# Cross-attention and gated FFN on one core: zero products during the first loads, another order of loads, and both ends of the attention reordered

## The chip, the core and the metric

The kernel runs on one core of one Trainium2 chip, in float32. The metric is the device time of one execution in microseconds; the number for the kernel before is the median of three runs, 1118.73 us (1117.19 to 1122.49). The engines are TensorE (PE; its weight loads are shown as PEld), VectorE (DVE), ScalarE (ACT), GpSimd (POOL) and SyncE (SP, which here only starts transfers). [...]

## The reference, cut to what matters

B = 8 blocks of S = 128 tokens, D = 512, H = 32 heads of 128; the FFN has 1376 inner columns.

```python
def reference(x, ctx_4096, mask_BxSxS2_bk0, position_bias, ln_weight, w_q, w_k, w_v, w_out, Wg, Wu, Wd, ag, au, ad):
    # hidden = layernorm(x)
    q = (rmsnorm(hidden) * ln_weight) @ w_q.T          # [B, S, 32, 128]
    k, v = ctx @ w_k.T, ctx @ w_v.T                    # [B, S, 32, 128]
    score = einsum('bqhd,bkhd->bhqk', q, k) + position_bias
    score = where(mask, softmax(where(mask, score, -inf)), 0)
    attn = einsum('bhqk,bkhd->bqhd', score, v)
    x = x + hidden + attn @ w_out.T
    # y = layernorm(x)
    x = x + ((silu((y @ Wg.T) * ag) * ((y @ Wu.T) * au)) @ Wd.T) * ad
```

## The kernel before

The 32 heads are worked on in NG = 8 groups of GH = 4 heads (512 columns). The host lays weights and context out with the contracted axis first. All large products are done by a seven-product scheme (Strassen-Winograd): each operand is cut into quarters, sums and differences of quarters are formed beforehand, and seven products of halves take the place of eight. `sums_a` (L220) and `sums_b` (L228) form the four sums of an operand, in place where they can. `combine_rows` (L236) does this on GpSimd for a group's weights, `token_sums` (L244) for the context and for the normalised tokens. `seven` (L259) runs the seven products for two output tiles each, so 14 steps, in the order 2, 1, 6, 7, 4, 5, 3. Products 2, 6, 7 and 4 are copied out of PSUM by ScalarE (L270, L280), products 1, 5 and 3 are added by VectorE (L275, L286). Product 6 accumulates into the bank of product 1, 7 into that of 6, 4 into that of 7, and 3 into that of 5: each must wait until the result before it has been read out of the bank. In the trace a matmul call in float32 shows as two records.

The stages follow one another on TensorE. First `kv(0, ...)` (L410) makes keys and values of group 0 in 28 steps while the loads come in; between the steps, at counts given by hand (L440 to L449), the blocks of x are normalised: `norm1_moments` (L186: statistics on VectorE, a square root on ScalarE), `norm1_scale` (L198: two small VectorE operations, the scaling on ScalarE) and `norm1_T` (L207: four transposes on TensorE, a multiplication on VectorE into hT). The sums of hT follow. Next come the queries of all eight groups (L541, L485 and L296), which are stored to DRAM. Then the attention runs over groups g = 0 to 7 and blocks b = 0 to 7. In each step `probabilities` (L327) adds position bias and mask on GpSimd into a tile s (three buffers, L332), makes the scores on TensorE (L337), adds them to s and takes the maximum on VectorE (L340 to L344), and makes four exponentials on ScalarE (L347) and the division on VectorE; `transpose_p` (L369) transposes in squares of 32 on VectorE and turns the rest with one store and four loads through DRAM (`turned`, then `pT`, all on SP's queue). Three steps later `attend` (L391) multiplies with the values, and ScalarE copies and stores the result (`att`). Between the steps TensorE makes three or four of the 28 steps of the next group's keys and values (`products`, counts at L687); before the first step it makes three. In group 7, whose successor has no keys, the steps of the output projection for the first two blocks (`first_out`, `out_products` at L618) stand in their place. `attended` (L605) loads a group's attended values for two blocks and forms their sums on VectorE; `load_wo` (L582) loads a group's rows of the output weights and forms their sums on GpSimd. Afterwards the output projection of the other three pairs of blocks follows, with residual and normalisation, and then the FFN.

A scheduler orders the instructions of each engine's queue by its own estimate of when each is ready, over what the program's order and the data allow; the hardware then works through each queue strictly in that order. Instructions given through `InOrder` (L37) are pinned behind whatever instruction was written just before them for the same engine. In the kernel before this holds for VectorE and GpSimd up to the queries, for TensorE during the first four steps of attention, and for TensorE and VectorE in group 7.

## Time and profile before

| what | value |
|---|---|
| median of three runs | 1118.73 us (1117.19 to 1122.49) |
| profiled execution | 1120.01 us, of it the program's span 1118.2 us |
| TensorE busy | 1093.8 us (98%), granted clock 0.997 over the span |
| VectorE, ScalarE, GpSimd busy | 571.4, 314.1, 373.7 us |
| group 0's keys and values | 4.4 to 63.9 us |
| queries | 63.9 to about 247 us |
| attention | 247 to about 761 us |
| rest of output projection, FFN | 761 to 1118 us |

A row of instructions gives the line, the engine, the operation, the tiles written and read, the shape and the count; in the order of time it begins with start and length in microseconds, and the brackets hold the idle time before it and what ended that. A row of waits says who waited for whom: microseconds in total, how often, and the longest. The chain of work that ended last is followed back from the end of the stretch asked for. A row of windows gives, for a stretch of time, its length and the busy time (and number) of PE, PEld, DVE, ACT and POOL, then the granted TensorE clock, the share of DMA and GB/s. TensorE counts as busy from the start of a matmul to its modelled end, so half speed looks busy too. SPq, ACTq and POOLq are the queues' own instructions, such as the start of a transfer.

### The profile page before, as it was taken

To read this page: it belongs to the slowest core of one execution; us is meant where nothing else is said; L and a number is where in the kernel's file an instruction comes from. 1 tells how busy PE (TensorE), PEld (TensorE's weight loads), DVE (VectorE), ACT (ScalarE), POOL (GpSimd) and SP (SyncE) were. 2 spreads that over 40 slices of the span, in tenths; PEclk is the share of its full clock that TensorE was granted. 3 is DMA by queue.
4 is the path that set the end of the run, shared out by engine and by line. 5 is a ranking of instruction groups with operands and counts; after the bars stand their busy time and mean duration, and the time that the engine had idled before them with its cause. 6 is when DMAs were issued, how large, how long until landed. Compare 5 with 4: busy or idle time off the path is not lost.

```text
span 1118.2 us, 13138 instructions
## 1 busy us (share of the span) xinstructions
PE 1093.8 (98%) x4526; PEld 775.1 (69%) x4526; DVE 571.4 (51%) x1122; ACT 314.1 (28%) x880; POOL 373.7 (33%) x386
## 2 busy tenths in 40 slices
PE   7999999998999999999999999998999999999998
PEld 4656666654868778685968778887888864444687
DVE  4664444436555565555555666643444333434732
ACT  2422211114444443434444344221000012223100
POOL 5283335535333333322311733620000316930010
PEclk9999999999999999999999999998999999999999
DMA  9113344448555555556545557664222512110011
GB/s 284 51 38 113 113 155 183 151 177 275 171 161 173 168 177 169 179 181 187 167 157 178 168 179 237 225 213 156 94 86 84 188 59 76 38 38 0 1 38 38
DMA packets 117538, 154.44 MB, mean 138 GB/s; under 512 B 12032, under 2 KB 71680, under 8 KB 117472
## 3 DMA queue, kind: packets, MB, share of 16 engines
q1 hardware_dynamic: 104416, 128.95, 36.2%
q10 hardware_dynamic: 11408, 18.88, 4.8%
q0 software_dynamic: 1648, 5.77, 1.6%
q8 instruction: 36, 0.59, 0.2%
q14 instruction: 30, 0.25, 0.1%
HBM read 101.14 MB, written 52.43 MB: 137 GB/s over the span
## 4 chain that ended last, share of the span: by engine, by line
PE 88%; DMA 4%; DVE 3%; POOL 2%; issue 1%; ACT 1%; SPq 0%; ACTq 0%; POOLq 0%; DVEq 0%
PE mm_v L314 16%; PE mm_k L296 14%; PE m L627 13%; PE mm_f L916 10%; PE mm_q L485 9%; PE d L995 6%; PE av L395 4%; PE sc L337 4%; PE ia_q L541 3%; PE ib_q L541 2%; PE mm_q L296 2%; DMA wo<-in_woT_dram 2%; DMA a<-att 1%; PE mm_k L45 1%; DMA wv<-in_wvT_dram 1%
## 5 line engine op out<-in xcount | busy, mean ns | idle before, releaser
L332 POOL TENSOR_TENSOR s<-pb,mneg 128x512 f32<-128x512 f32 x64 | 81.4, 1275 | 274.1 <-DVE tt L372 228.9
L314 PE MATMUL mm_v<-wv,ctx_sb 128*128 128x256 f32 x512 | 118.2, 379 | 1.4 <-DMA wv<-in_wvT_dram 1.4
L296 PE MATMUL mm_k<-ctx_sb,wk 128*128 128x512 f32 x224 | 105.0, 602 | 6.5 <-DMA wk<-in_wkT_dram 4.4
L347 ACT ACTIVATE s<-s,nmx 128x128 f32<-128x128 f32 x252 | 98.0, 390 | 44.6 <-DVE nmx L344 29.5
L314 PEld LDWEIGHTS mm_v<-wv,ctx_sb 128*128 128x128 f32 x512 | 94.5, 190 | 14.4 <-DMA wv<-in_wvT_dram 2.2
L314 PE MATMUL mm_v<-S_v,ctx_sb 128*128 128x256 f32 x384 | 86.6, 380 | 3.3 <-DVE v L45 1.7
L400 ACT COPY aT<-av 128x512 f32<-128x512 f32 x64 | 37.5, 587 | 183.2 <-PE av L395 142.1
L314 PEld LDWEIGHTS mm_v<-S_v,ctx_sb 128*128 128x128 f32 x384 | 71.9, 190 | 14.1 <-DVE v L45 2.3
L296 PE MATMUL mm_k<-ctx_sb,S_k 128*128 128x512 f32 x168 | 75.1, 592 | 0.0
L627 PE MATMUL m<-wo,a 128*128 128x256 f32 x300 | 74.3, 386 | 0.0
L337 PEld LDWEIGHTS sc<-k,q 128*128 128x128 f32 x416 | 58.7, 191 | 20.2 <-issue 18.2
L340 DVE TENSOR_TENSOR s<-sc,s 128x512 f32<-128x512 f32 x56 | 38.7, 691 | 65.3 <-PE sc L337 61.1
L296 PEld LDWEIGHTS mm_k<-ctx_sb,wk 128*128 128x128 f32 x224 | 40.4, 193 | 44.4 <-issue 34.8
L493 ACT COPY q<-mm_q 128x512 f32<-128x512 f32 x56 | 31.4, 588 | 121.5 <-PE mm_q L485 111.8
L627 PEld LDWEIGHTS m<-wo,a 128*128 128x128 f32 x300 | 57.6, 194 | 7.8
L545 DVE TENSOR_TENSOR q<-q,ia_q 128x256 f32<-128x256 f32 x84 | 34.9, 421 | 52.6 <-PE ia_q L541 51.7
L337 PE MATMUL sc<-k,q 128*128 128x128 f32 x416 | 59.0, 275 | 0.0
L296 PEld LDWEIGHTS mm_k<-ctx_sb,S_k 128*128 128x128 f32 x168 | 31.2, 190 | 35.4 <-issue 34.0
L395 PE MATMUL av<-pT,v 128*128 128x128 f32 x416 | 55.0, 275 | 0.0
L485 PE MATMUL mm_q<-hT,S_q 128*128 128x512 f32 x112 | 52.3, 592 | 0.0
L485 PE MATMUL mm_q<-hT,wq 128*128 128x512 f32 x112 | 52.3, 592 | 0.0
L395 PEld LDWEIGHTS av<-pT,v 128*128 128x128 f32 x416 | 50.6, 192 | 0.0
(251 smaller groups left out, 1940.7 us busy)
## 6 DMA issues: line engine op xcount, KB each, us to landing
queries<-q SPq DMA_DIRECT2D x32, 512.0 KB, 3.5
q<-queries SPq DMA_DIRECT2D x32, 512.0 KB, 4.8
turned<-tt SPq DMA_DIRECT2D x64, 256.0 KB, 2.1
pT<-turned SPq DMA_DIRECT2D x256, 64.0 KB, 2.6
att<-aT ACTq DMA_DIRECT2D x64, 256.0 KB, 3.1
a<-att SPq DMA_DIRECT2D x24, 512.0 KB, 3.3
wq<-in_wqT_dram SPq DMA_DIRECT2D x8, 1024.0 KB, 5.3
wk<-in_wkT_dram SPq DMA_DIRECT2D x7, 1024.0 KB, 6.2
```

The costliest lines, as they stand in the source:

```text
L296: kv_tensor.matmul(out, w[i][:, c, bass.ts(t, P)], src[i][:, c, :], start=(first and c == 0), stop=(c == HC - 1), skip_group_check=True,)
L314: kv_tensor.matmul(out[:, bass.ts(k, HW)], src[i][:, c, bass.ts(2 * t + k, S)], w[i][:, c, :], start=(first and k == 0 and c == 0), stop=( ...
L332: nc.gpsimd.tensor_tensor(s, pb, mneg[:, b : b + 1, :].to_broadcast([P, GH, S]), ALU.add)
L337: tensor.matmul(sc[:, j, :], qT[:, j, bass.ts(b % 2, S)], kT[j][:, cols], start=True, stop=True)
L340: vector.tensor_tensor(s, sc, s, ALU.add)
L347: (InOrder(tc, nc.scalar) if (g, b) == (0, 0) else nc.scalar).activation(s[:, j, :], s[:, j, :], AF.Exp, bias=nmx[:, j : j + 1], accum_out ...
L395: tensor.matmul(av[:, j, :], v[b // 2][:, b % 2, bass.ts(j, P)], pT[:, :, j, :], start=True, stop=True,)
L485: nc.tensor.matmul(m[t], w[i][:, c, bass.ts(t, P)], h_t[i][:, c, :], start=(i in (1, 5) and c == 0), stop=(c == HC - 1), skip_group_check= ...
L541: nc.tensor.matmul(m, a[n][i], b[n][i], start=i in (2, 1, 5), stop=True, skip_group_check=True)
L627: tensor.matmul(m[n], sa[n][:, c, :], wo_t[g][n][:, c, :], start=(g == order[0] and c == 0 and k % 2 == 0), stop=(g == order[-1] and c == ...
L916: nc.tensor.matmul(out, ws[t][n][:, c, :], h2_t[n][:, c, :], start=(first and c == 0), stop=(c == HC - 1), skip_group_check=True,)
L995: nc.tensor.matmul(out, lhs, rhs, start=bank not in started, stop=(i == NP - 1 or n == 8), skip_group_check=True,)
```

## The change

At the start, eight products of a zero tile (128x128 by 128x256, into a PSUM bank of its own) are written before everything else of TensorE. The first loads come in another order: the values' weights are issued right behind the first keys' weights, and the second half of the keys' weights moves from ACT's queue to SP's, ahead of x. Keys and values of group 0 are written in the order two steps of keys, two of values, two of keys, two of values, and the values' sums only after that. ScalarE's copies and normalisations up to the queries are pinned in the order in which they are written, and the normalisation's counts change.

At the start of attention two steps of products (not three) precede the first scores, three follow each of the first six blocks, and four follow the last two. The loads of wo for groups 0 and 1 are pinned on SP behind what is written before them at groups 1 and 2, and their sums are written at block 3 of groups 1, 2 and 6.

In group 7 GpSimd and SP are pinned too. The masked bias is made two blocks ahead; attended values are loaded one block ahead from SP instead of POOL; one step of the last values' products moves between the exponentials and the sums; wo's sums are written one block after its load, and the last wo is loaded at block 4 instead of 5. The attended values of the second pair of blocks for groups 0 and 1 are loaded and summed (on GpSimd) at the end of group 7, and the first four of their seven products are written around the last two `attend`s, into banks that attention leaves. The other three follow afterwards.

```diff
@@ -132,13 +132,14 @@
     for c in (2, 3):
         nc.scalar.dma_start(wk0[:, c, lo], wkT[bass.ts(c, P), lo])
         nc.sync.dma_start(ctx_sb[:, c, :512], ctxT[bass.ts(c, P), :512])
+    load_part(nc.scalar, wv0, wvT, 1, lo)
     load_part(nc.scalar, wk0, wkT, 0, lo)
     load_part(nc.sync, ctx_sb, ctxT, 0, slice(0, 512))
+    load_part(nc.scalar, wv0, wvT, 0, lo)
     for fh in (1, 0):
-        load_part(nc.scalar, wv0, wvT, fh, lo)
         load_part(nc.sync, ctx_sb, ctxT, fh, slice(512, T))
-        load_part(nc.scalar, wk0, wkT, fh, hi)
     for fh in (1, 0):
+        load_part(nc.sync, wk0, wkT, fh, hi)
         load_part(nc.scalar, wv0, wvT, fh, hi)
     kv_w = {0: (wk0, wv0)}
     x_in = [acts.tile([P, 2, D], F32, tag="a", name=f"x_{i}") for i in range(B // 2)]
@@ -147,7 +148,14 @@
     q_w = {0: load_q(0)}
-    vector, gpsimd = InOrder(tc, nc.vector), InOrder(tc, nc.gpsimd)
+    vector, gpsimd, scalar = (InOrder(tc, e) for e in (nc.vector, nc.gpsimd, nc.scalar))
+    zeros = work.tile([P, 256], F32, tag="aT", name="zeros")
+    nc.vector.memset(zeros, 0.0)
+    zero = ps.tile([P, 256], F32, tag="av", name="zero")
+    for _ in range(8):
+        nc.tensor.matmul(zero, zeros[:, :P], zeros, start=True, stop=True)
     lnw_sb = const.tile([P, DC], F32, name="lnw_sb")
     nc.gpsimd.dma_start(lnw_sb, lnw.rearrange("(c p) -> p c", p=P))
...
@@ -192,7 +200,7 @@
         rr = small.tile([P, 1], F32, tag="rr", name=f"rr_{b}")
         vector.tensor_scalar(rr, mv1[:, b, 1:2], 1.0 + EPS, EPS * EPS, ALU.mult, ALU.add)
+        scalar.activation(rr, rr, AF.Sqrt)
         return b, rr
...
+            scalar.copy(part(1, 1, t), m[t])
             yield
...
@@ -324,14 +332,17 @@
         yield from seven(name, range(2), product, part, *banks)
-    def probabilities(g, b, qT, kT, pb, between=None):
+    def masked_bias(eng, g, b, pb):
+        s = work.tile([P, GH, S], F32, tag="s", name=f"s_{g}_{b}", bufs=3)
+        eng.tensor_tensor(s, pb, mneg[:, b : b + 1, :].to_broadcast([P, GH, S]), ALU.add)
+        return s
+    def probabilities(g, b, qT, kT, pb, between=None, s=None):
         cols = bass.ts(b, S)
         n = f"{g}_{b}"
-        s = work.tile([P, GH, S], F32, tag="s", name=f"s_{n}", bufs=3)
-        nc.gpsimd.tensor_tensor(
-            s, pb, mneg[:, b : b + 1, :].to_broadcast([P, GH, S]), ALU.add
-        )
+        if s is None:
+            s = masked_bias(nc.gpsimd, g, b, pb)
         sc = ps.tile([P, GH, S], F32, tag="sc", name=f"sc_{n}")
         for j in range(GH):
             tensor.matmul(
@@ -418,13 +429,17 @@
             yield from project_V(f"v{g}", combine_rows(f"v{g}", wv), ctx_t, v, ps_mm)
         else:
+            rows_v = {1: wv[:, :HC, :HW], 2: wv[:, HC:, :HW]}
+            values = project_V(f"v{g}", rows_v, ctx_t, v, ps, "sc")
+            yield from itertools.islice(keys, 2)
+            yield from itertools.islice(values, 2)
             ctx_sums[0]()
-            yield from itertools.islice(keys, 3)
+            yield from itertools.islice(keys, 1)
             ctx_sums[1]()
             ctx_sums[2]()
             yield from itertools.islice(keys, 1)
-            values = project_V(f"v{g}", combine_rows(f"v{g}", wv), ctx_t, v, ps, "sc")
-            yield from itertools.islice(values, 4)
+            rows_v.update(combine_rows(f"v{g}", wv))
+            yield from itertools.islice(values, 2)
             ctx_sums[3]()
             yield from keys
             yield from values
@@ -437,11 +452,11 @@
     h_t, h_sums = token_sums(hT)
     scales = []
     for n, _ in enumerate(kv(0, kvs)):
-        if n in (3, 6, 8, 9, 10, 12, 14, 16):
+        if n in (6, 7, 8, 9, 10, 12, 14, 16):
             scales.append(norm1_moments(len(scales) + len(normed) + transposed1))
-        if n in (6, 8, 9, 10, 12, 14, 16, 18):
+        if n in (8, 9, 10, 11, 12, 14, 16, 18):
             normed.append(norm1_scale(*scales.pop(0)))
-        if n in (10, 11, 12, 14, 16, 18, 20, 22):
+        if n in (10, 11, 12, 13, 14, 16, 18, 20):
             norm1_T(*normed.pop(0))
             transposed1 += 1
...
+    scalar = nc.scalar
     res_scale = const.tile([P, B], F32, name="res_scale")
     res_bias = const.tile([P, B], F32, name="res_bias")
@@ -581,54 +597,77 @@
     def load_wo(g):
         src = woT[bass.ts(g, GW), :].rearrange("(c p) n -> p c n", p=P)
...
+            sync.dma_start(w, src)
...
-        wo_t[g] = sums_b(
-            nc.gpsimd, up[:, :, :HW], up[:, :, HW:], dn[:, :, :HW], dn[:, :, HW:], t1, t2, t4
-        )
-    def attended(g, i):
+        def sums(eng):
+            wo_t[g] = sums_b(
+                eng, up[:, :, :HW], up[:, :, HW:], dn[:, :, :HW], dn[:, :, HW:], t1, t2, t4
+            )
+        return sums
+    def load_att(g, i, eng):
         a = acts.tile([P, 2, GH, S], F32, tag="a", name=f"a_{g}_{i}")
-        (nc.sync if i else nc.gpsimd).dma_start(a, att[g][i])
+        eng.dma_start(a, att[g][i])
+        return a
+    def att_sums(g, i, a, eng):
         s = acts.tile([P, 3, HC, S], F32, tag="a", name=f"S_a{g}_{i}")
         return sums_a(
-            vector, a[:, 0, :HC], a[:, 0, HC:], a[:, 1, :HC], a[:, 1, HC:],
+            eng, a[:, 0, :HC], a[:, 0, HC:], a[:, 1, :HC], a[:, 1, HC:],
             s[:, 0], s[:, 1], s[:, 2],
         )
+    def attended(g, i):
+        return att_sums(g, i, load_att(g, i, nc.sync), nc.vector)
+    PRODUCTS = (1, 2, 6, 7, 4, 5, 3)
     def by_product(banks):
-        return {n: banks[k // 2][:, k % 2, :] for k, n in enumerate((1, 2, 6, 7, 4, 5, 3))}
-    def out_products(i, order, banks, fetched):
+        return {n: banks[k // 2][:, k % 2, :] for k, n in enumerate(PRODUCTS[: 2 * len(banks)])}
+    def out_product(g, sa, m, order, names=PRODUCTS):
+        for n in names:
+            for c in range(HC):
+                tensor.matmul(
+                    m[n], sa[n][:, c, :], wo_t[g][n][:, c, :],
+                    start=(g == order[0] and c == 0 and PRODUCTS.index(n) % 2 == 0),
+                    stop=(g == order[-1] and c == HC - 1), skip_group_check=True,
+                )
+    def out_products(i, order, banks, fetched, begun=0):
         m = by_product(banks)
-        for at, g in enumerate(order):
+        for names in ((4, 5), (3,)):
+            for g in order[:begun]:
+                out_product(g, fetched[g], m, order, names)
+        for g in order[:begun]:
+            del fetched[g]
+            yield
+        for at in range(begun, NG):
+            g = order[at]
             sa = fetched.pop(g)
             if i and at + 1 < NG:
                 fetched[order[at + 1]] = attended(order[at + 1], i)
-            for k, n in enumerate((1, 2, 6, 7, 4, 5, 3)):
-                for c in range(HC):
-                    tensor.matmul(
-                        m[n], sa[n][:, c, :], wo_t[g][n][:, c, :],
-                        start=(g == order[0] and c == 0 and k % 2 == 0),
-                        stop=(g == order[-1] and c == HC - 1), skip_group_check=True,
-                    )
+            out_product(g, sa, m, order)
             yield
@@ -655,13 +694,14 @@
             kv_w[g + 2] = load_kv(g + 2)
         if g + 1 < NG:
             products = kv(g + 1, kvs)
-        if g in (1, 2):
-            load_wo(g - 1)
-        if g == NG - 2:
-            load_wo(2)
+        if g in (1, 2, NG - 2):
+            wo_sums = load_wo(min(g - 1, 2))
         if g == NG - 1:
             tensor, vector = InOrder(tc, nc.tensor), InOrder(tc, nc.vector)
-            fetched = {}
+            fetched, next_fetched = {}, {}
+            gpsimd, sync, wo_sums = InOrder(tc, nc.gpsimd), InOrder(tc, nc.sync), None
+            biased = [masked_bias(gpsimd, g, k, pb) for k in range(2)]
+            come = {(0, 0): load_att(0, 0, sync)}
         for b in range(B):
             if b % 2 == 0:
                 qT = ahead.pop((g, b // 2))
@@ -671,21 +711,36 @@
             if (g, b) == (0, 0):
                 tensor = kv_tensor = InOrder(tc, nc.tensor)
-                for _ in range(3):
+                for _ in range(2):
                     next(products)
             if g == NG - 1:
-                p = probabilities(
-                    g, b, qT, kT, pb, lambda: fetched.update({b: attended(b, 0)})
-                )
+                if b + 2 < B:
+                    biased.append(masked_bias(gpsimd, g, b + 2, pb))
+                if b + 1 < B:
+                    come[b + 1, 0] = load_att(b + 1, 0, sync)
+                if b + 2 >= B:
+                    come[b + 2 - B, 1] = load_att(b + 2 - B, 1, sync)
+                if wo_sums:
+                    wo_sums = wo_sums(gpsimd)
+                def between():
+                    if b == 0:
+                        next(products)
+                    fetched[b] = att_sums(b, 0, come.pop((b, 0)), vector)
+                p = probabilities(g, b, qT, kT, pb, between, biased.pop(0))
             else:
                 p = probabilities(g, b, qT, kT, pb)
+                if g in (1, 2, NG - 2) and b == 3:
+                    wo_sums(InOrder(tc, nc.gpsimd))
             pend.append((g, b, transpose_p(g, b, p), v))
             advance(3)
-            if (g, b) != (0, 0):
-                for _ in range(4 if b % 2 and (g < NG - 2 or b == 3) else 3):
-                    next(products, None)
+            more = b > 5 if g == 0 else b % 2 and (g < NG - 2 or b == 3)
+            for _ in range(4 if more else 3):
+                next(products, None)
             if (g, b) == (0, 3):
                 tensor = kv_tensor = nc.tensor
             if g == NG - 1:
@@ -698,15 +753,28 @@
...
-                if b < NG - 4 or b == 5:
-                    load_wo(b + 3 if b < NG - 4 else NG - 1)
+                if b < NG - 3:
+                    wo_sums = load_wo(b + 3)
                 if b:
                     next(first_out)
+                if b + 2 >= B:
+                    n = b + 2 - B, 1
+                    next_fetched[n[0]] = att_sums(*n, come.pop(n), gpsimd)
+    BEGUN = 2
+    second = list(range(NG))
+    second_banks = [ps.tile([P, 2, HW], F32, tag="sc", name=f"m{k}_1") for k in range(2)]
     advance(2)
     next(first_out)
+    for g in second[:BEGUN]:
+        out_product(g, next_fetched[g], by_product(second_banks), second, PRODUCTS[:4])
+        if g == 0:
+            advance(1)
     advance(0)
-    fetched[0] = attended(0, 1)
-    tensor, vector = nc.tensor, nc.vector
+    second_banks += [ps.tile([P, 2, HW], F32, tag="av", name=f"m{k}_1") for k in (2, 3)]
+    next_fetched[BEGUN] = attended(second[BEGUN], 1)
+    fetched = next_fetched
+    tensor, vector, gpsimd = nc.tensor, nc.vector, nc.gpsimd
     attn.close()
@@ -781,10 +849,12 @@
     for i in range(1, B // 2):
         last = i + 1 == B // 2
         order = [2, 3, 4, 5, 6, 7, 0, 1] if last else list(range(NG))
-        banks = [ps.tile([P, 2, HW], F32, tag="m", name=f"m{k}_{i}") for k in range(4)]
-        if i > 1:
-            fetched[order[0]] = attended(order[0], i)
-        for n, _ in enumerate(out_products(i, order, banks, fetched)):
+        if i == 1:
+            banks, begun, ps.n = second_banks, BEGUN, 4
+        else:
+            banks = [ps.tile([P, 2, HW], F32, tag="m", name=f"m{k}_{i}") for k in range(4)]
+            fetched[order[0]], begun = attended(order[0], i), 0
+        for n, _ in enumerate(out_products(i, order, banks, fetched, begun)):
             if n in (2, 3):
                 norm2_T(*ys[n - 2])
         m = by_product(banks)
```

More of the change, by code (lines that the diff above doesn't have):

```diff
@@ L194, in norm1_moments @@
         vector.tensor_scalar(rr, mv1[:, b, 1:2], 1.0 + EPS, EPS * EPS, ALU.mult, ALU.add)
-        nc.scalar.activation(rr, rr, AF.Sqrt)
+        scalar.activation(rr, rr, AF.Sqrt)
         return b, rr
@@ L203, in norm1_scale @@
         hn = work.tile([P, D], F32, tag="pT", name=f"hn_{b}", bufs=4)
-        nc.scalar.activation(hn, xb, AF.Identity, bias=nm, scale=rr)
+        scalar.activation(hn, xb, AF.Identity, bias=nm, scale=rr)
         return b, hn
@@ L269, in seven @@
             product(2, t, m[t], True)
-            nc.scalar.copy(part(1, 1, t), m[t])
+            scalar.copy(part(1, 1, t), m[t])
             yield
@@ L279, in seven @@
                 product(i, t, m[t], False)
-                nc.scalar.copy(part(r, c, t), m[t])
+                scalar.copy(part(r, c, t), m[t])
                 yield
@@ L583, in load_wo @@
         src = woT[bass.ts(g, GW), :].rearrange("(c p) n -> p c n", p=P)
+        sync = InOrder(tc, nc.sync)
         if g == NG - 1:
@@ L587, in load_wo @@
             )
-            nc.sync.dma_start(up, src[:, :HC])
-            nc.sync.dma_start(dn, src[:, HC:])
+            sync.dma_start(up, src[:, :HC])
+            sync.dma_start(dn, src[:, HC:])
             t1, t2, t4 = (
@@ L595, in load_wo @@
             w = (wpool if held else wos).tile([P, GH, D], F32, tag="w", name=f"wo{g}")
-            nc.sync.dma_start(w, src)
+            sync.dma_start(w, src)
             t = (spool if held else wos).tile(
@@ L600, in load_wo @@
             up, dn, t1, t2, t4 = w[:, :HC], w[:, HC:], t[:, 0], t[:, 1], t[:, 2]
-        wo_t[g] = sums_b(
-            nc.gpsimd, up[:, :, :HW], up[:, :, HW:], dn[:, :, :HW], dn[:, :, HW:], t1, t2, t4
+        def sums(eng):
[4 more added lines that the diff above has]
+    def load_att(g, i, eng):
+        a = acts.tile([P, 2, GH, S], F32, tag="a", name=f"a_{g}_{i}")
+        eng.dma_start(a, att[g][i])
+        return a
@@ L603, in load_wo @@
+    def att_sums(g, i, a, eng):
+        s = acts.tile([P, 3, HC, S], F32, tag="a", name=f"S_a{g}_{i}")
+        return sums_a(
+            eng, a[:, 0, :HC], a[:, 0, HC:], a[:, 1, :HC], a[:, 1, HC:],
+            s[:, 0], s[:, 1], s[:, 2],
         )
     def attended(g, i):
-        a = acts.tile([P, 2, GH, S], F32, tag="a", name=f"a_{g}_{i}")
-        (nc.sync if i else nc.gpsimd).dma_start(a, att[g][i])
-        s = acts.tile([P, 3, HC, S], F32, tag="a", name=f"S_a{g}_{i}")
-        return sums_a(
-            vector, a[:, 0, :HC], a[:, 0, HC:], a[:, 1, :HC], a[:, 1, HC:],
-            s[:, 0], s[:, 1], s[:, 2],
-        )
```

## The prediction

> **What bounds it now.** I read the page's shares and chain first, then the list of what TensorE waited for, then the order of time around each wait.
>
> ```profile
> PE 1093.8 (98%) x4526; PEld 775.1 (69%) x4526; DVE 571.4 (51%) x1122; ACT 314.1 (28%) x880; POOL 373.7 (33%) x386
> ...
> PE 88%; DMA 4%; DVE 3%; POOL 2%; issue 1%; ACT 1%; SPq 0%; ACTq 0%; POOLq 0%; DVEq 0%
> ```
>
> TensorE is the bound, and the change removes none of its work: all it can give back is TensorE's idle time and half-speed time. The list of its waits says how much idle time there is (us in total, times, longest):
>
> ```profile
> PE mm_k L296 <- DMA wk<-in_wkT_dram: 4.4, 1, 4.4
> PE av L45 <- DMA pT<-turned: 3.1, 1, 3.1
> PE mm_k L45 <- ACT k L280: 3.0, 2, 1.7
> PE mm_k L296 <- ACT k L280: 2.2, 1, 2.2
> PE mm_v L314 <- DVE v L45: 1.7, 1, 1.7
> PE mm_v L314 <- POOL s L45: 1.6, 1, 1.6
> PE mm_v L314 <- DMA wv<-in_wvT_dram: 1.4, 1, 1.4
> ...
> PE mm_k L45 <- DVE k L286: 1.2, 2, 0.8
> PE m L45 <- DMA a<-att: 0.9, 2, 0.6
> PE m L45 <- DVE S_a L45: 0.3, 1, 0.3
> ```
>
> With one wait of the FFN (1.4) the list adds up to 21.2 us. Nearly all of it lies in three stretches: 0 to 64 us (group 0's keys and values), 247 to 283 (the first steps of attention) and 686 to 762 (its last group). The queries (64 to 247) and the middle of attention (283 to 686) show a TensorE without waits, so time won before them reaches the end.
>
> **Part A, the start.** TensorE and ScalarE in order of time (start, length):
>
> ```profile
> 4.37 5.28 PE L296 MATMUL mm_k<-ctx_sb,wk 128*128 128x512 f32 x8 [4.37 <-DMA wk<-in_wkT_dram]
> 11.03 3.72 PE L314 MATMUL mm_v<-wv,ctx_sb 128*128 128x256 f32 x16 [1.39 <-DMA wv<-in_wvT_dram]
> ...
> 28.07 0.81 ACT L204 ACTIVATE hn<-x,nm,rr 128x512 f32<-128x512 f32 x1 [1.16 <-DVE nm L45]
> 28.80 0.56 ACT L280 COPY k<-mm_k 128x512 f32<-128x512 f32 x1
> 29.41 1.98 PE L296 MATMUL mm_k<-ctx_sb,wk 128*128 128x512 f32 x4 [2.18 <-ACT k L280]
> ```
>
> Eight records of 128x512 take 3.44 us later on; here they take 5.28: about 1.8 us go to a slow clock. Then values wait for their weights. Loads move some 0.36 MB/us here (373 GB/s between 10 and 20 us). The new order puts the 256 KB of wv after 768 KB of keys' operands, the first of which had landed at 4.37, so wv is there by an estimated 5.1 (0.7 us later) and the 1.4 us wait goes. SP gets two issues of wk ahead of x's eight, ScalarE two fewer of nine; x's first load (11.01 now) goes out about as before, for it waits for landings, not for its turn.
>
> The zeros cost time as well. A call shows as two records: 16 of 128x256, 0.216 us each at full clock (16 in 3.46), 0.43 at half. Begun at about 1.2 (first queue entries at 0.75 plus a memset), they last 6.9 us at half clock: to 8.1, past the 4.37 at which real work could start. The trace's nearest row is the half-speed stretch after the wait at 756:
>
> ```profile
> 758.50:765.30 6.80, 5.85 (x18) 5.07 (x19) 6.15 (x18) 2.07 (x3) 1.10 (x1) 0.50 0.91 329
> ```
>
> Granted clock 0.50 for 6.8 us, though TensorE worked again from 759.45. [...] By the row (6.8 us from 1.2) the gain is nothing. If zeros did not count as activity at all, the keys would run cold from 8.1 (5.28) and the values end at 16.9: a loss of 2.1. I take 0.8.
>
> ScalarE's order: the copy at 28.80, which frees the bank that TensorE wants at 27.1, stood behind a normalisation whose inputs VectorE had late. In program order the second such copy stands behind the square roots of three blocks and the scaling of one; VectorE must do about 6.6 us for them after TensorE's seventh product (two value adds 1.3, three moments 3.0, a token sum 1.8, a scaling 0.5), while TensorE does three products (5.2) and can begin the fourth. So 1.5 to 2 us of the 2.2 can return: what is late next is the same copy, held by VectorE. I take 0.8 gained, between 2.2 and a loss of 3 (VectorE slower at each of the following copies). The wait at 58 (1.6) is a value add on VectorE behind token sums that GpSimd's work stretched (one takes 2.46 us, others 0.42); that code is unchanged, two transposes come earlier: 0.6. A: **2.2**, from -5 to 5.
>
> **Part B, attention begins.** The chain there:
>
> ```profile
> 253.18 7.97 DMA wo<-in_woT_dram
> ...
> 271.98 1.28 POOL s L332
> ...
> 275.73 0.60 DVE k L286
> 276.46 1.97 PE mm_k L45 x4
> ```
>
> GpSimd does eight sums of wo (261.28 to 271.69) which nobody needs before 690, and the bias of a block waits behind them; VectorE's add, two key adds behind it, and TensorE (0.4 + 0.8) follow. The two waits for ScalarE (3.0) have four exponentials of each of two blocks ahead of a copy: both blocks' scores stand next to each other. Now three products (5.2 us) lie between scores; exponentials (1.6) and copies (0.6 each) then fit. Of 4.2 us waited, with pipeline refill 4.8, I take **3.8**, from 0 to 4.8. The wo load and sums go to groups 1 and 2: the load is pinned on SP behind the load of the next values (335.29 now), so landing at about 347 after two transfers; four sums of 1.27 are 5.1 us on GpSimd. Behind them there stand the sums of wv (343.77, first used at 354) and later blocks' biases, which have 15 us (a bias of 319.5 is added at 336). Hidden, or, if wv's sums come second, 347 + 5.1 + 2.5 = 354.6, late by 0.6 once or twice.
>
> **Part C, attention ends.** GpSimd, VectorE and TensorE:
>
> ```profile
> 733.18 1.28 POOL L230 TENSOR_TENSOR wo<-wo 128x512 f32<-128x512 f32 x1 [7.47 <-DMA wo<-in_woT_dram]
> ...
> 742.19 0.42 DVE L45 TENSOR_TENSOR S_a<-a 128x256 f32<-128x256 f32 x1 [7.56 <-DMA a<-att]
> ...
> 759.45 2.05 PE L45 MATMUL av<-pT,v 128*128 128x128 f32 x8 [3.10 <-DMA pT<-turned]
> ```
>
> The load of attended values stood in GpSimd's queue behind wo sums that waited for their own load; VectorE, in order, stood 7.56 us for it, and the last block's softmax moved back by as much. Hence 3.1 us idle, and nine records at half clock behind it, 0.21 each, 1.9. The change issues that load a block ahead from SP, and has 16 x 2 records (6.9 us) of the second output product to run before the last attend: 6.9 covers 3.3 even if VectorE stays late, and the clock keeps. The v wait (1.9 with refill) goes as one value product moves ahead of the sums; small waits 0.5 + 0.5 + 0.75 go with the load. Sum 1.9 + 1.75 + 3.3 + 0.2 + 1.9 = 9.0; I take **8.0**, from 2 to 9.
>
> Its price elsewhere: the wo load waits on SP behind pT (issued some 9.6 us after a block's scores), lands 4.4 to 7 later, the sums end by 22, the bias that follows is wanted four blocks (31) later: 9 us to spare. Two groups' attended sums, eight of about 0.7 us, move to GpSimd and hide under the output products. [...]
>
> **Sum.** 2.2 + 3.8 + 8.0 = 14.0 off a span of 1118.2: 1104.2, and with 1.8 around it 1106.0 for the profiled execution of 1120.0. That one lies 1.3 above the median of 1118.7, so **1104.7**.
>
> **Rivals.** (1) The end alone, and half of it: VectorE holds ScalarE's strict order at the start (A -2), the first steps refill their waits with exponentials (B 2), C 5: 1113.7. For it: VectorE is 9.6 of 10 us busy from 20 to 30. Against: B's and C's causes stand in two chains. (2) The waits only move: each bank is freed as late as before; 1118.7. For it: copies still follow VectorE; against: 6.9 us of new cover in C. (3) Slower, by GpSimd's and SP's strict order in the last group: a wo load that uses up the 9 us to spare holds the sums, the biases behind them, and so the scores. Five loads, each late by e beyond it, cost 5e and C's gain: with e = 5, 25 - 6 = 19 slower, 1137. It decides from e = 2.3 (a landing of 16 to 18 us against 4.4 to 7) on; more than 0.5% slower from 3.4.
>
> **Numbers.** A measurement tells about 0.5% (5.6 us) from no change. Mine 0.70 (1100 to 1111), rival 1 0.15, rival 2 0.08, rival 3 0.07. Half of rival 1 still lies below 1113.1: faster 0.77, same 0.16, slower 0.07. The range leaves out rival 2, rival 3 and a little at the bottom: 1099 to 1116.
>
> **What would show it.** TensorE: no wait for wv near 9.5; queries from about 61.5 instead of 63.9; no wo sum on GpSimd before 340; no wait for k between 247 and 283; last attend without a wait and no granted clock of 0.5 after 700. Wrong if the wait for k's copy grows, if GpSimd waits for wo in the last group with VectorE behind it, or if the zeros run on past 8.

## The result, and the profile after

The changed kernel takes 1115.23 us (median of 20 runs, 1112.5 to 1116.94) where the kernel before takes 1120.82 beside it (20 runs, 1116.74 to 1123.29): a ratio of 0.9947, 95% interval 0.9940 to 0.9955. It is 5.6 us faster, not 14.0. The profiled execution has a span of 1115.2 us, against 1118.2. It was the slowest of the twenty (1116.94), so the profiles compared below show 3.0 of the 5.6 us.

The page of the changed kernel, busy time and the chain's shares, answers to the first view shown of before:

```profile
PE 1098.3 (98%) x4542; PEld 779.7 (70%) x4542; DVE 579.7 (52%) x1115; ACT 313.8 (28%) x880; POOL 377.0 (34%) x386
...
PE 92%; DMA 3%; DVE 3%; ACT 1%; issue 1%; SPq 1%; ACTq 0%; DVEq 0%
```

TensorE is still the bound; the sixteen more records are the zeros. Its waits in the changed kernel (us in total, times, longest):

```profile
PE mm_k L45 <- DVE k L283: 3.2, 1, 3.2
PE m L45 <- DMA a<-att: 3.0, 2, 2.3
PE m L45 <- DVE v L45: 2.2, 1, 2.2
PE tp L187 <- ACT hn L45: 1.2, 1, 1.2
PE zero L158 <- DVE zeros L155: 1.2, 1, 1.2
PE mm_f L986 <- DVE act L45: 1.1, 1, 1.1
PE mm_k L45 <- ACT k L288: 0.9, 2, 0.6
PE mm_k L304 <- POOL ctx_sb L45: 0.6, 1, 0.6
```

The list has fallen from 21.2 to 13.4 us. The waits for pT, wv and GpSimd's value sums are gone, and so are the 4.4 us for wk (1.2 for the zeros stand there now). The first three rows are new or grown, and two of them are followed by half clock (a granted clock of 0.50). Windows of the changed kernel (length; PE, PEld, DVE, ACT, POOL busy; then clock, DMA share, GB/s):

```profile
254.50:261.35 6.85, 5.70 (x13) 3.54 (x14) 2.33 (x5) 0.59 (x1) 1.27 (x1) 0.50 0.24 77
735.80:739.20 3.40, 3.40 (x9) 2.71 (x9) 3.40 (x3) 0.00 (x0) 3.40 (x4) 0.50 0.36 108
```

To see where time went, I cut every profiled execution at the same four instructions: first query product, first product of group 1's values in attention, first scores of the last group, first transpose after the output projection's first half. Lengths in us:

| profiled execution | A: start to queries | B: queries to values | middle | C: last group to transposes | rest |
|---|---|---|---|---|---|
| before | 63.7 | 219.1 | 399.8 | 98.9 | 336.8 |
| changed | 60.9 | 221.6 | 399.5 | 96.7 | 336.5 |
| gained | 2.8 | -2.5 | 0.3 | 2.2 | 0.3 |
| forecast | 2.2 | 3.8 | 0 | 8.0 | 0 |

A came about as forecast, B turned into a loss, and C gave a quarter. The start of the changed kernel (start, length; TensorE):

```profile
1.20 5.76 PE L158 MATMUL zero<-zeros 128*128 128x256 f32 x16 [1.20 <-DVE zeros L155]
6.79 3.60 PE L304 MATMUL mm_k<-ctx_sb,wk 128*128 128x512 f32 x8
10.22 3.62 PE L322 MATMUL mm_v<-wv,ctx_sb 128*128 128x256 f32 x16
...
60.91 3.60 PE L501 MATMUL mm_q<-hT,wq 128*128 128x512 f32 x8
```

The zeros end before 7.0, the keys run in 3.60 instead of 5.28 us, and the values do not wait for wv.

**B in the changed kernel.** The chain that leads to TensorE's wait, cut at 257 us (start, length, what):

```profile
250.58 0.18 DVE nmx L355
...
250.82 1.28 ACT L45
...
252.12 1.66 ACT s L45 x8
...
253.80 0.18 DVE ri L365
...
254.83 0.69 DVE k L283
...
255.65 2.04 PE mm_k L45 x2
```

TensorE in order of time there, and the same key add in the kernel before, where VectorE makes it ahead of the first scores' addition:

```profile
248.86 3.60 PE L45 MATMUL mm_k<-ctx_sb,wk 128*128 128x512 f32 x8
255.65 3.75 PE L45 MATMUL mm_k<-ctx_sb,S_k 128*128 128x512 f32 x4 [3.19 <-DVE k L283]
...
252.74 0.69 DVE L275 TENSOR_TENSOR k<-k,mm_k 128x512 f32<-128x512 f32 x1 [4.72 <-PE mm_k L45]
253.64 0.69 DVE L340 TENSOR_TENSOR s<-sc,s 128x512 f32<-128x512 f32 x1 [0.21 <-PE sc L45]
```

Read the chain backwards. TensorE's product 6 accumulates into the bank of product 1, so it needs the key add, `k L283`. VectorE made that add only at 254.83, although the product that it reads was finished before 251 (the first four of eight records begun at 248.86). It stands behind block 0's division, which waited for a table load (1.28) and four exponentials (1.66, two records each) on ScalarE. In the kernel before three key products stood ahead of the first scores, so this add was made before the softmax; now two stand there, and the third comes behind it.

**C in the changed kernel**, the chain at the first blocks of the last group:

```profile
681.60 2.01 DMA turned<-tt
...
684.96 0.43 SPq L390
...
685.49 3.66 DMA a<-att
...
689.17 0.44 DVE S_a L45
```

The first attended load, a_0_0, is pinned on SP; the four pT loads of the block before stand ahead of it and wait for their own transfer. In the kernel before, GpSimd's queue issued a_0_0 at 676.44. Now it goes out at 685.49 and lands at 689.15; VectorE has waited 3.62 us for it, and behind it stand the division and the two value adds that TensorE wants before the output products (what these adds read is finished by 689.2). First the load of before, then the adds and the product of the changed kernel:

```profile
676.44 0.58 POOL L608 DMA_DIRECT2D a<-att  x1
...
692.42 1.25 DVE L45 TENSOR_TENSOR v<-v,mm_v 128x512 f32<-128x512 f32 x2
693.12 1.99 PE L45 MATMUL m<-wo,a 128*128 128x256 f32 x8 [2.16 <-DVE v L45]
```

Later in the same group, in order of time:

```profile
725.89 0.43 SPq L45 DMA_DIRECT2D wo<-in_woT_dram  x1
...
726.42 0.60 SPq L45 DMA_DIRECT2D a<-att  x1
...
734.86 0.42 DVE L45 TENSOR_TENSOR S_a<-a 128x256 f32<-128x256 f32 x1 [2.86 <-DMA a<-att]
734.88 2.90 PE L45 MATMUL m<-wo,a 128*128 128x256 f32 x8 [2.34 <-DMA a<-att]
```

An attended load goes out right behind a wo load of 1 MB and lands 8.4 us later, where the median of this kernel's is 5.4 and the quickest 3.7.

### The profile page after: what moved, and what is told of

It is laid out like the page before. It is cut to its first block, busy times and chain, and to the rows that moved or that the text cites. A ratio compares the mean times of both kernels' runs of the same rounds, so it can differ in the third digit from the quotient of the medians.

```text
span 1115.2 us, 13161 instructions
## 1 busy us (share of the span) xinstructions
PE 1098.3 (98%) x4542; PEld 779.7 (70%) x4542; DVE 579.7 (52%) x1115; ACT 313.8 (28%) x880; POOL 377.0 (34%) x386
## 4 chain that ended last, share of the span: by engine, by line
PE 92%; DMA 3%; DVE 3%; ACT 1%; issue 1%; SPq 1%; ACTq 0%; DVEq 0%
PE mm_v L322 16%; PE mm_k L304 15%; PE m L649 12%; PE mm_f L986 10%; PE mm_q L501 9%; PE d L1065 6%; PE av L406 4%; PE sc L348 4%; PE ia_q L557 3%; PE m L45 3%; PE ib_q L557 2%; PE mm_q L304 2%; DMA a<-att 2%; PE mm_k L45 1%; DMA turned<-tt 1%; PE tp L187 1%
## 5 line engine op out<-in xcount | busy, mean ns | idle before, releaser
L337 POOL TENSOR_TENSOR s<-pb,mneg 128x512 f32<-128x512 f32 x56 | 71.1, 1270 | 259.3 <-DVE tt L383 239.6
L649 PE MATMUL m<-wo,a 128*128 128x256 f32 x276 | 66.8, 379 | 0.0
L649 PEld LDWEIGHTS m<-wo,a 128*128 128x128 f32 x276 | 52.0, 190 | 6.8
```

The costliest lines, as they stand in the source:

```text
L337: eng.tensor_tensor(s, pb, mneg[:, b : b + 1, :].to_broadcast([P, GH, S]), ALU.add)
L649: tensor.matmul(m[n], sa[n][:, c, :], wo_t[g][n][:, c, :], start=(g == order[0] and c == 0 and PRODUCTS.index(n) % 2 == 0), stop=(g == ord ...
```

## The experiments

Ratios are to the kernel before, measured anew beside each group of runs; its medians were 1121.12, 1121.48 and 1120.08 us in the three groups. Every run has its granted clock on record. Edits are to the changed kernel unless said.

### The parts alone

`start_only` is the kernel before with part A: the order of loads, the zeros, ScalarE's order, the order of keys and values and the normalisation's counts. Of its edit, for instance:

```diff
-    vector, gpsimd = InOrder(tc, nc.vector), InOrder(tc, nc.gpsimd)
+    vector, gpsimd, scalar = (InOrder(tc, e) for e in (nc.vector, nc.gpsimd, nc.scalar))
+    zeros = work.tile([P, 256], F32, tag="aT", name="zeros")
...
-        if n in (3, 6, 8, 9, 10, 12, 14, 16):
+        if n in (6, 7, 8, 9, 10, 12, 14, 16):
```

> Only the start is changed (zero products, order of loads, ScalarE's order up to the queries); both ends of attention are as before. Theory: the start gives what its stretch shows in the trace, queries begin at about 60.9 instead of 63.7, 2.8 us, and it reaches the end: about 1118.0 us against 1120.8, ratio 0.9975. Rival (the start's gain is lost again because attention's first steps wait for something with a fixed time): 1120.5, ratio 1.000. Rival (the start is all of the change's gain, the ends give nothing): 1115.2.

Measured: 1118.17 us, 0.9967 (0.9951 to 0.9984), 3 to 4 us off. Queries begin at 60.9, and B is 219.1 long as before. So A is worth what its stage shows, and it is not A that spoils B. (The profiled execution, 1114.46, is among the four quickest of its twelve, the ones with a granted clock of 1.000; it had no half clock after the start, so its C of 96.4 is not used.) No run has part B alone.

`no_zeros` has the changed kernel without its zero products:

```diff
-    for _ in range(8):
+    for _ in range(0):
         nc.tensor.matmul(zero, zeros[:, :P], zeros, start=True, stop=True)
```

> The changed kernel without the eight products of zeros, all else alike. If the zeros are worth their time (full clock when the keys begin): the first keys' eight records take 5 us or more from 4.4, the values follow at 9.7 to 11.4 instead of 10.2, and the time is 0 to 1.2 us above the changed kernel's 1115.2. If they are a cost (the real work could have opened the clock by itself and starts 2.4 us earlier): values from 9.7, up to 0.5 us below 1115.2.

Measured: 1119.09 us, 0.9971 (0.9957 to 0.9985). Its start:

```profile
4.38 6.78 PE L304 MATMUL mm_k<-ctx_sb,wk 128*128 128x512 f32 x8 [4.38 <-DMA wk<-in_wkT_dram]
10.99 3.62 PE L322 MATMUL mm_v<-wv,ctx_sb 128*128 128x256 f32 x16
```

The keys took 6.78 us instead of 3.60; yet the values begin only 0.8 us later than with zeros, and the queries 0.3 (61.2): the waits that follow take up the rest. Of the 3.9 us between the two medians only 0.3 therefore lie in the start. In this profile C is 98.5, with a half clock of 6.8 us from 693.3 on, which begins within a wait of 3.8 us for v. The granted clock is 0.9956 on average of these twelve runs and 0.9971 of the changed kernel's twenty: an estimated 1.7 us more lost at half speed. Why, and where the rest goes, stays open.

`end_only` has part C alone: the changed kernel with the start of before, and with part B undone too (the load of wo for groups 0 to 2 unpinned, its sums where they stood, the counts of products as before).

```diff
-            wo_sums = load_wo(min(g - 1, 2))
+            load_wo(min(g - 1, 2))(nc.gpsimd)
...
-                for _ in range(2):
+                for _ in range(3):
                     next(products)
...
-                if g in (1, 2, NG - 2) and b == 3:
-                    wo_sums(InOrder(tc, nc.gpsimd))
```

> The kernel before with the reordered end of attention alone (the last group and what follows it); the start and the begin of attention as before. By the two profiles the end gained 2.4 us, so 1118 to 1119 where the kernel before is at 1121. If the end is worth the 8.0 us of the forecast and only the begin of attention spoils it, 1113.

Measured: 1121.49 us, 1.0006 (0.9989 to 1.0022): nothing, less than either number expected. The wait for the value adds is 4.5 us here, and C 98.3. By the medians part C alone, as written, pays as much as it gives.

### Part B: the add behind the softmax

`key_add_first` leaves two products ahead of the first scores and writes two more, with their key adds on VectorE, between block 0's exponentials and its division:

```diff
-                p = probabilities(g, b, qT, kT, pb)
+                first = (g, b) == (0, 0)
+                vector = InOrder(tc, nc.vector) if first else nc.vector
+                p = probabilities(
+                    g, b, qT, kT, pb, (lambda: (next(products), next(products))) if first else None
+                )
...
-            for _ in range(4 if more else 3):
+            for _ in range(1 if (g, b) == (0, 0) else 4 if more else 3):
```

> The changed kernel with the additions of product 1 of the keys ahead of the first block's division in VectorE's queue (two of the three steps after the first scores are written between the exponentials and the division). Theory: the wait of 3.2 us at 252 goes, and with it the half clock that follows it (3 to 3.4 us when it strikes): 4 to 6.5 us below 1115.2, so 1109 to 1111, granted clock 1.0 from 245 to 290. Rival (the exponentials with their table load hold the next copies and a wait of the same size appears there): 1113 to 1115.

Measured: 1110.94 us, 0.9901 (0.9881 to 0.9921), B 215.9 instead of 221.6. In order of time:

```profile
251.09 1.28 ACT L45 ACT_TABLE_LOAD   x1 [2.07 <-DVE nmx L45]
251.10 0.69 DVE L45 TENSOR_TENSOR k<-k,mm_k 128x512 f32<-128x512 f32 x1
252.56 1.88 PE L45 MATMUL mm_k<-ctx_sb,S_k 128*128 128x512 f32 x4
```

The add runs while ScalarE loads its table, and product 6 starts without a wait. The profiled execution is the quickest of only four (1108.54), and its C is shorter too (93.5) though nothing was changed there; the gain to go by is that of the medians, 4.3 us. `counts_as_before` tests the same from the other side: three products ahead of the scores again.

```diff
-                for _ in range(2):
+                for _ in range(3):
                     next(products)
...
-            more = b > 5 if g == 0 else b % 2 and (g < NG - 2 or b == 3)
-            for _ in range(4 if more else 3):
-                next(products, None)
+            if (g, b) != (0, 0):
+                for _ in range(4 if b % 2 and (g < NG - 2 or b == 3) else 3):
+                    next(products, None)
```

> The changed kernel with the kernel before's counts of key products at the begin of attention: three ahead of block 0's scores, none behind its softmax, four at every odd block. The third product's add then stands on VectorE ahead of the softmax. If the new count alone cost the begin of attention, the stretch from the queries to the first value product is 219 us as in the kernel before, not 221.6, and the time about 1112.7. If the exponentials and copies kept in order and the sums elsewhere cost it, the stretch stays at 221 to 222 and the time at 1115.

Measured: 1111.10 us, 0.9913 (0.9893 to 0.9933), B 216.3. That is 2.8 better than the 219.1 of before, so the rest of part B (wo's loads and sums elsewhere) does give most of the 3.8; the new counts alone cost 5.3 of B, of which 2.6 are the half clock (see the next run). The time fell further than the 1112.7 that the stage of before would give, because B fell below the 219 that I had expected.

`zeros_in_wait` fills the wait with eight zero products and takes nothing away:

```diff
+                if (g, b, n) == (0, 0, 2):
+                    zeros = work.tile([P, 256], F32, tag="aT", name="zeros_1")
+                    nc.vector.memset(zeros, 0.0)
+                    zero = ps.tile([P, 256], F32, tag="av", name="zero_1")
+                    for _ in range(8):
+                        tensor.matmul(zero, zeros[:, :P], zeros, start=True, stop=True)
                 next(products, None)
```

> As the changed kernel, with eight more products of zeros on TensorE just ahead of the sixth key product of the begin of attention, where it waits 3.2 us for VectorE's key add; no wait is taken away. If the half clock after that wait costs as much as the wait itself (6.8 us at half speed, 3.4 us lost), the clock is full after it and the time falls by 2 to 3 us, to about 1112.5. If the half clock there is no consequence of the idle, nothing changes: 1115.

Measured: 1115.46 us, 0.9951 (0.9933 to 0.9969): no gain. In its profile the place looks as hoped:

```profile
252.12 3.62 PE L45 MATMUL zero<-zeros 128*128 128x256 f32 x16
255.58 1.88 PE L45 MATMUL mm_k<-ctx_sb,S_k 128*128 128x512 f32 x4
```

Product 6 takes 1.88 instead of 3.75 us, and B is 219.0, 2.6 shorter. But the middle is 1.5 longer (waits of 0.7 and 0.5 us that the changed kernel didn't have, both for copies on ScalarE) and C 1.2. And `first_att_early` below, with the same 3.2 us wait and no zeros, had no half clock there and a B of 219.0 too. So the half clock behind this wait comes in some executions only. Filling the wait is worth nothing that I could measure; removing it is worth 4.

### Part C: who stands ahead of the attended loads

`att_loads_on_act` issues the attended loads of the last group from ScalarE's queue, pinned:

```diff
-            come = {(0, 0): load_att(0, 0, sync)}
+            loads = InOrder(tc, nc.scalar)
+            come = {(0, 0): load_att(0, 0, loads)}
...
-                    come[b + 1, 0] = load_att(b + 1, 0, sync)
+                    come[b + 1, 0] = load_att(b + 1, 0, loads)
...
-                    come[b + 2 - B, 1] = load_att(b + 2 - B, 1, sync)
+                    come[b + 2 - B, 1] = load_att(b + 2 - B, 1, loads)
```

> The changed kernel with the loads of attended values in the last group started from ScalarE's queue instead of SP's, where each stands behind a load of wo (1 MB). Theory: landing falls from about 8 us to 3 to 5, TensorE's waits for these loads (2.3 + 0.7) and the half clock after the first of them (1.7) go, and the wait for a value add at 691 (2.2) shrinks because the first of these loads comes earlier: 4 to 7 us below 1115.2, 1108 to 1111. Rival (VectorE is late in this group because GpSimd's sums run beside its own, 1.4 us instead of 0.4 for each): the waits stay near their size, 1114 to 1115.

Measured: 1115.65 us, 0.9948 (0.9930 to 0.9966). The waits for a and v are gone from its list, and this one has come:

```profile
PE av L45 <- DMA pT<-turned: 3.6, 1, 3.6
```

SP's queue ahead of that wait:

```profile
733.90 0.97 SPq L45 DMA_DIRECT2D wo<-in_woT_dram  x2
735.63 0.34 SPq L385 DMA_DIRECT2D turned<-tt  x1
743.23 1.96 SPq L390 DMA_DIRECT2D pT<-turned  x4
```

The store of the turned probabilities now stands right behind the wo loads, its four loads go out 7.6 us later, and 6.8 us of half clock follow the wait. By the medians that costs as much as was won.

`wo_unpinned` gives the wo loads of the last group to SP without a fixed place:

```diff
-        sync = InOrder(tc, nc.sync)
+        sync = InOrder(tc, nc.sync) if g < 3 else nc.sync
```

> As the changed kernel, but the six loads of the last group's 1 MB blocks of wo are given to SP's queue without being held to their written place, so the scheduler may let them go early, as in the kernel before; the loads of attended values keep their place. Theory 'behind a megabyte' (an attended load lands 8 us after its issue because the wo load stands just ahead of it in SP's queue): the two waits m<-wo,a on DMA a<-att (2.3 + 0.7 us) go, and the half clock behind the longer one (about 1.7 us) with them, so 3 to 5 us below the changed kernel, about 1111. Rival 'the load itself is slow in this stage': the waits stay wherever the wo loads stand, 1115.

Measured: 1117.28 us, 0.9963 (0.9949 to 0.9977), if anything slower than the changed kernel: both theories missed. The two waits for a did go, though single attended loads still took up to 7.7 us; but the wait for v grew to 6.3 us. Its chain shows why:

```profile
681.07 5.54 DMA turned<-tt
...
688.52 4.27 DMA a<-att
...
692.81 0.44 DVE S_a L45
```

A wo load had floated to 680.00, just ahead of the turned store of 681.07. That store took 5.54 us instead of 2.01, pT followed it, and a_0_0, pinned behind pT, went out 3 us later still. This run named the second cause.

`first_att_early` moves only that load back to GpSimd's queue, unpinned:

```diff
-            come = {(0, 0): load_att(0, 0, sync)}
+            come = {(0, 0): load_att(0, 0, nc.gpsimd)}
```

> As the changed kernel, but the first attended load, a_0_0, alone goes out from GpSimd's queue unheld, as in the kernel before. Theory: it lands before the last group's first block, the VectorE sum S_a of block 0 no longer waits 3.6 us for it, the two value adds behind that sum are not late, and the wait m<-wo,a on DVE v (2.2 us) and any half clock behind it go: 2 to 4 us below the changed kernel, about 1112. Rival: the wait for v comes from VectorE's order of the value adds alone and stays near 2 us: 1115.

Measured: 1113.00 us, 0.9924 (0.9903 to 0.9944), with C 91.9 instead of 96.7. The same places in order of time:

```profile
668.65 0.58 POOL L628 DMA_DIRECT2D a<-att  x1 [0.84 <-PE av L406]
...
683.82 0.42 DVE L45 TENSOR_TENSOR S_a<-a 128x256 f32<-128x256 f32 x1
...
687.05 1.25 DVE L45 TENSOR_TENSOR v<-v,mm_v 128x512 f32<-128x512 f32 x2
...
689.14 1.89 PE L45 MATMUL m<-wo,a 128*128 128x256 f32 x8
```

The sum, the value adds and the output product follow each other without a wait. The 2.2 us wait came from the queue of that one load.

### Together

`keys_first` joins `key_add_first` and `first_att_early`.

> The changed kernel with two places moved: two of block 0's key products and the first key add ahead of block 0's softmax division, and a_0_0 alone from GpSimd's queue unheld. If the two late places are separate causes, their gains add: the add's place alone stood 4.3 us below the changed kernel, the load's place alone 2.2, so about 1108.7, and by stage the queries to the first value product 216 us, block 56's scores to the first transpose of y 92 us. If each gain came from the same thing (which windows of the clock are low), the sum is no better than the better one, 1111.

Measured: 1107.96 us, 0.9886 (0.9864 to 0.9908); B 215.9, C 92.3. The gains (4.3 and 2.2) add, to within 1 us: two causes. The granted clock is 1.000 in all six runs, against 0.9971 on average of the changed kernel's twenty, so by estimate up to 3.2 of the 7.3 us gained are half clock that no longer comes. Its largest wait left in C is `m` for an attended load, 1.3 us.

`keys_wo_first` adds the edit of `wo_unpinned` to it.

> As keys_first, with the wo loads of the last group not held to their place on SP as well. With a_0_0 out of SP's way an early wo load can no longer stand ahead of it; if the later attended loads are then freed of the wo loads ahead of them, 1 to 2 us below keys_first, about 1107; if the waits for attended loads are only moved to the copies of the turned probabilities, as when the loads stood on ScalarE's queue, the same as keys_first, 1108.7.

Measured: 1103.10 us, 0.9844 (0.9823 to 0.9866); B 215.9, C 88.6. TensorE's whole list of waits:

```profile
PE mm_k L45 <- ACT k L288: 1.5, 2, 0.9
PE tp L187 <- ACT hn L45: 1.2, 1, 1.2
PE zero L158 <- DVE zeros L155: 1.2, 1, 1.2
PE mm_f L990 <- DVE act L45: 1.0, 1, 1.0
PE mm_k L304 <- POOL ctx_sb L45: 0.6, 1, 0.6
```

Between 283 and 900 us none is left. The edit that by itself gained nothing, or cost 2 us, gains 4.9 here. Two reasons can be seen, and no run separates them: a_0_0 no longer stands on SP, where an early wo load held it up by 3 us in `wo_unpinned`; and of the unpinned wo loads three now go out 0.4 us behind an attended load (at 693.04, 702.03 and 711.12) instead of just ahead of one. `keys_wob_first` instead writes each wo load behind its block's attended load, still pinned:

```diff
                 if wo_sums:
                     wo_sums = wo_sums(gpsimd)
+                if 0 < b < NG - 2:
+                    wo_sums = load_wo(b + 2)
...
-                if b < NG - 3:
-                    wo_sums = load_wo(b + 3)
```

> As keys_first, with each wo load of the last group written behind the attended load of its block instead of ahead of it, still held to its place on SP, and its sums on GpSimd one block later. If the attended load is late by the megabyte ahead of it, 1 to 2 us below keys_first, about 1107; if GpSimd's sums of wo come too late for the products by the shift, new waits m<-T_o for POOL appear and it is above keys_first, 1110 or more.

Measured: 1106.09 us, 0.9869 (0.9848 to 0.9890), C 90.2, with one wait of 1.1 us left before an output product. The five attended loads that here go out ahead of a wo load landed after 3.3 to 4.5 us; in `keys_first` the three that go out 0.5 us behind one took 5.4 to 8.1. Turning the two loads round gives 1.9 us over `keys_first`, as that theory said. But a place ahead of wo is not always enough: in the changed kernel an attended load left at 686.54, 0.7 us ahead of a wo load, and took 7.2 us. `keys_wo_first`, 17.0 us below the kernel before, is the best version.

## Why the prediction was right or wrong

**Part A held.** Queries at 60.9 against "about 61.5", no wait for wv, zeros over before 8. Its terms shifted among themselves. The 0.8 that I took for zeros and loads was an estimate that no run shows; the changed kernel showed 0.9 (values' sixteen records end at 13.84, not 14.75). ScalarE's order, taken at 0.8, gave about 0.2: TensorE's lost time of 2.35 us near 27, refill included, became 0.78 and 1.39. The value add near 58, taken at 0.6, gave its whole 1.74. The row of the kernel before that I had for the slow clock (half speed for 6.8 us, so until 8.0) was a poor guide: a weight load took 0.34 us until 5.1 and 0.19 from 5.5 on, so the full clock came at about 5.4.

**Part B failed at one sentence**, "Now three products (5.2 us) lie between scores". That is true, and the waits on ScalarE fell as it says (from 3.0 to 0.9 us). But I priced what stands on ScalarE's queue between the scores and not what stands on VectorE's: moving the third product behind the first scores moved its key add behind a softmax. My own list of what would show it had "no wait for k between 247 and 283"; the trace has 3.2 us there. The other term that I left out is the half clock behind a wait of that size: 2.6 us where it comes (B is 221.6 with it and 219.0 without, with the same wait). With the add's place mended, B is 215.9, a gain of 3.2 where I had 3.8.

**Part C failed at two sentences.** "The change issues that load a block ahead from SP" took the early issue as a gain for every attended load. For a_0_0 it is the reverse: it came from GpSimd's queue at 676.44 and now stands behind pT on SP. I followed what SP's order does to wo, and not what it does to the first load. So "The v wait (1.9 with refill) goes" failed, although one value product was moved as said: the adds are late because VectorE waits in front of them. The second is that the small waits "go with the load". A load pinned behind 1 MB of wo landed after 8.4 us, and 0.9 us of waits for a became 3.0. I had looked at wo as the one that waits ("9 us to spare", and that did hold: no wait for wo's sums appeared), not as the one that others wait for. What held is the last attend: the 3.1 us wait for pT and its half clock are gone. I had put that half clock at 1.9; at half speed for 5.85 us behind the wait it was 2.9. The 8.0 has no term for sums that VectorE and GpSimd make at the same time. Single attended sums on VectorE that ran beside sums on GpSimd took up to 1.49 us in the changed kernel and 1.52 in `keys_wo_first`, where others took 0.42. In the kernel before two of a block's four were that long (1.38 at 694.78, 1.49 at 696.09; 3.6 for the four), in the worst blocks of these two kernels three or all of them: 4.6 and 5.7 us for the four. TensorE waits for none of it in `keys_wo_first`.

The rivals: the second (waits only move) describes most of what happened, with A on top; the first had the size nearly right (1113.7) for other reasons, since A was not what failed. The third did not occur (its last threshold was also miscounted: by its own sum 0.5% slower begins at e = 2.3, and 3.4 is 1%). With both failed steps of C and the one of B mended (`keys_wo_first`), the stages gain 2.9, 3.2 and 10.2 us, so the 14.0 was there; the change as written did not collect it.

What stays open: why the half clock follows the same wait in one execution and not in the next, why `no_zeros` loses most of its 3.9 us behind the start, and where the 2.6 us of `zeros_in_wait` go. The profile of `no_zeros` shows other waits and half clocks, that of `zeros_in_wait` other waits at a granted clock of 1.000: no common cause.

## What to carry to other kernels

When a step is moved past another, write down for each engine which of its instructions change places, not only for the engine whose wait you want to remove: here an add of 0.69 us that moved behind a softmax took back all that the rest of the reordering gave in that stage. The pinned a_0_0 went out 9 us later than before, because of what stood ahead of it in its queue, and an attended load pinned right behind a wo load landed after 8.4 us, where the median was 5.4; so ask both questions of every pinned load, the first one of a series above all. And test two repairs together before judging either: unpinning wo gained nothing while a_0_0 stood on SP, and gained 4.9 once it did not.

## What the runs showed of the hardware

After the start and before the last microseconds, the half clock (0.50) came in one stretch of 6.8 us in the kernel before (from 758.5) and in stretches of 6.8 and 3.4 us in the changed kernel (from 254.5 and 735.8). In these two profiles no TensorE wait of up to 2.2 us was followed by one. Waits of 2.3 us (at 732.5 in the changed kernel) and 2.5 us (`key_add_first`) were, one of 2.6 us in `zeros_in_wait` was not (a granted clock of 1.000 over its span), and the same wait of 3.2 us was followed by 6.8 us in the changed kernel, by 3.4 in `no_zeros` and by none in `first_att_early`.

The full clock came while TensorE had made nothing but products of zeros: in the changed kernel a weight load took 0.34 us until 5.1 us and 0.19 from 5.5 on, and the first product of real data begins at 6.79. Without zeros weight loads took 0.34 us until 7.4 and 0.19 from 7.8 on in the kernel before, and in `no_zeros` the first keys' eight records took 6.78 us from 4.38 on instead of 3.60; if the 3.18 us more are all half speed, the full clock came there at 10.7, an estimate.

A store of 256 KB took 5.5 instead of 2.0 us behind a 1 MB load that left the same queue 1.1 us earlier (`wo_unpinned`), and 6.3 in the kernel before, also 1.1 us behind such a load (682.12 behind 681.02).
